# Attention with a depthwise convolution on one core: key stacks on another DMA queue, and query and key parts made at other points

## The chip, the cores and the metric

The kernel runs on one core of one Trainium2 chip. The metric is the device time of one execution in microseconds (us). A core has engines that run on their own and meet at semaphores: TensorE (PE in the profile; its weight loads are PEld), VectorE (DVE), ScalarE (ACT), GpSimd (POOL) and SyncE (SP). SP only issues DMA transfers; ScalarE and GpSimd can issue them too, each on its own queue.

## The reference

```
B, C, H, W = 4, 384, 48, 48;  N = 2304;  8 heads of 48
local   = batchnorm(depthwise_conv7x7(x))              # per channel
q, k, v = layernorm(x) @ qkv_w.T + qkv_b               # over channels, per token
q       = q + layernorm(local)
attn    = softmax(q @ k.T * 48**-0.5)                  # per head, 2304 x 2304
out     = x + (attn @ v) @ proj_w.T + proj_b           # in the layout of x
```

## The kernel before

**Tiling.** An image's 2304 tokens are cut into 6 groups of 384 tokens (8 rows of 48 pixels). There are 24 groups in all, t = 0 to 23, image b = t // 6, group g = t % 6. Heads are taken in 4 pairs; a pair fills 128 partitions, 64 for each head. Channels 0 to 287 in packed form give pairs 0 to 2, and the fourth pair is gathered from the 16 last rows of each half of the three chunks, the "tails".

**A group** is 12 slots, s = 0 to 11. Slot s belongs to pair s // 3 and to third s % 3 of the keys. `score_batch` makes six score blocks (key blocks of 128 by 384 queries) with three products for each head, and `nc.scalar.activation` takes their exponential; `weigh_batch` multiplies the six blocks with the values and sums them. The sums are copied out of PSUM by ScalarE (`sums_out`) and added by VectorE one slot later (`sums_add`). All products, scores and sums share four PSUM buffers of two banks.

**Scores from two parts.** Queries and keys are split into a high part, rounded to the faster format, and the low part that is left. For a query pair, `high_queries` casts on ScalarE (L745), `low_queries` subtracts on VectorE (L750), and SP then copies rows within the tile `qs` (L755, L757) so that 64 partitions hold the wanted combination. For keys, `stacks[b, p]` (tile `ks`, two buffers) is a pair's stack of 2 x 2304 columns. In the first group of an image the stack of the next pair is put together from the DRAM tensor `keys` by eight transfers (`stack_head`), and `keep_stack` writes the finished stack to DRAM (`wide`). In later groups `load_keys` reads it back in three pieces of 768 KB, one in each slot of the pair before. All these are issued on ScalarE's queue, after the six exponentials of the slot.

**The convolution** is 147 VectorE instructions for each group (49 taps times 3 chunks, L288). It runs one group and more ahead, in small portions between the other work: `convolve(...)` issues the portion that `plan` gave to that point. `plan` shares the instructions out by the room that `spare` and `spare_at_keys` state for each half slot, and by due points: all of group t's convolution must be issued by the first norm slot of group t - 1.

**The norm of the next group's queries** goes through slots too: `norm_slots(t)` gives (first, second), which are (6, 9) for t > 0 and (8, 10) for t = 0. The sum over channels is made one slot before `first` and sent out through DRAM (`parts`, `four`), the mean is taken off in `first`, squares are summed in the slot after it, the variance comes in `second`, and in slot `second + 1` stand `local_end` and `query_end`, which finish the queries in `xn`; `query_end` ends with `gather_tails`, eight small SP transfers into `qt`. Behind it, in the same slot, come `high_queries(t + 1, 0)` and, after the slot's second convolution portion, `low_queries(t + 1, 0)`. For the other pairs both stand in the middle slot (third 1) of the pair before.

**Before images 1 to 3** there is a key stage ("kv"), in which `from_x` makes values, keys and queries of the image's six groups and, beside them, the output projections of the image before. It is a generator; `both` takes two steps of it, the products of two items and then what reads them. For a key, the second step casts the high part on ScalarE (L592), makes the low part on VectorE (L593) and issues its transfers. The first part of the program (the prologue) does the same for image 0.

**Order.** TensorE, VectorE and ScalarE execute in the order of the program text. The orders on SP and GpSimd are set by the framework's scheduler.

Of the kernel before, what the change touches and what calls it, by code (L numbers as in the profile page):

```python
# [24 lines left out]
BATCH = 6  # L25
# [20 lines left out]
def unshifted_pass(  # L46
# [263 lines left out]


    def norm_slots(t):
        return (6, 9) if t else (8, 10)

    def spare(t, s, half):
        b, g = divmod(t, NG)
        first, second = norm_slots(t)
        time = 3.6 - (0.0 if half else 0.6) - (0.6 if half and s % 3 == 1 else 0.0)
        if b + 1 < B and g >= later(b + 1):
            time -= {(3, 1): 2.3, (4, 1): 2.2, (5, 1): 2.3, (7, 0): 0.4, (8, 0): 2.6}.get(  # L320
                (s, half), 0.0
            )
        if g:
            time -= {(2, 0): 0.7, (4, 1): 1.4}.get((s, half), 0.0)
        if t == 0:
            time -= {(7, 1): 1.1, (8, 1): 1.4, (9, 1): 1.1, (11, 0): 5.0}.get((s, half), 0.0)
        elif t + 1 < NT:
            time -= {(5, 1): 2.3, (6, 1): 2.2, (7, 1): 2.3, (9, 0): 0.4, (10, 0): 4.5}.get(
                (s, half), 0.0
            )  # L330
        return max(0.3, time)
# [37 lines left out]
    def convolve(*point):  # L369
        for _ in range(share[point]):  # L370
            next(stream)
# [143 lines left out]
                )  # L515

    keys, values = {}, {}

    def keys_out(b, g, u, k):
        at = slice(g * G, (g + 1) * G)  # L520
# [26 lines left out]

    def keep_stack(b, p):
        wide[b, p] = dram.tile([P, 2, N], F32, tag=f"wide{p}", name=f"wide{b}_{p}")
        nc.scalar.dma_start(out=wide[b, p], in_=stacks[b, p].bitcast(F32))  # L550

    def load_keys(b, p, i):
        if i == 0:
            place_keys(b, p)
        if (b, p) in wide:
            at = slice(i * BATCH * P, (i + 1) * BATCH * P)
            nc.scalar.dma_start(
                out=stacks[b, p].bitcast(F32)[:, :, at], in_=wide[b, p][:, :, at]
            )
        elif i == 0:  # L560
            for j in range(2):
                stack_head(b, p, j, keys[b][2 * p + j], slice(0, N), nc.scalar)

    def from_x(b, g, before=None, ao=None):


        src = xn[b, g]
        flat = big.tile([P, NB * NH * HA + 64 - HA], F32, tag=f"v{g}", name=f"v{b}_{g}")
        v = flat[:, 0 : NB * NH * HA].rearrange("p (t h d) -> p t h d", t=NB, h=NH)
        values[b, g] = flat  # L570
        if g == 0:
            keys[b] = dram.tile([NH, HD, 2, N], F32, tag="keys", name=f"keys{b}")
        nc.gpsimd.memset(v[:, :, :, HD:HA], 1.0)
        nc.gpsimd.memset(flat[:, NB * NH * HA :], 0.0)
        queries_of_group = []

        def value(blk, r):
            project(
                r[:, :C],
                lambda c: src[:, c, blk * P : (blk + 1) * P],  # L580
                lambda c: w_v[:, c, :],
            )
            yield
            nc.scalar.copy(v[:, blk, :, 0:HD], r[:, :C].rearrange("p (h d) -> p h d", d=HD))  # L584
            yield

        def key(u, r):
            project(r[:, :G], lambda c: w_qk[:, c, 1, u, :], lambda c: src[:, c, :])
            yield
            bias = qkb[:, 1, u : u + 1]  # L590
            k = work.tile([P, 2, G], HALF, tag="pt", name=f"k{b}_{g}_{u}", bufs=5)
            nc.scalar.activation(k[:, 0, :], r[:, :G], AF.Identity, bias=bias)  # L592
            nc.vector.scalar_tensor_tensor(  # L593
                k[:, 1, :], r[:, :G], bias, k[:, 0, :], ALU.add, ALU.subtract
            )
            keys_out(b, g, u, k)
            yield

        def query(u, r):
            project(r[:, :G], lambda c: w_qk[:, c, 0, u, :], lambda c: src[:, c, :])  # L600
            queries_of_group.append(r)
            yield
            if u == CC - 1:
                for i, q in enumerate(queries_of_group):
                    nc.scalar.activation(  # L605
                        src[:, i, :], q[:, :G], AF.Identity, bias=qkb[:, 0, i : i + 1]
                    )
            yield

        def output(co, r):  # L610
            project(r[:, :G], lambda c: w_o[:, c, co * P : (co + 1) * P], lambda c: ao[:, c, :])
            yield
            finish(before, co, r[:, :G])
            yield

        todo = [(value, i) for i in range(NB)] + [(key, i) for i in range(CC)]
        todo += [(query, i) for i in range(CC)]
        if ao is not None:
            todo += [(output, i) for i in range(CC)]
        while todo:  # L620
            r = two_banks()
            steps = [f(i, r[:, j, :]) for j, (f, i) in enumerate(todo[:2])]
            todo = todo[2:]
            for _ in range(2):
                for step in steps:
                    next(step)
                yield

    def both(making):
        next(making)  # L630
        next(making)


# [90 lines left out]
    def query_end(t):  # L724

        acc = accs.pop(t)
        q = xn[divmod(t, NG)]
        q3 = work.tile([P, G], F32, tag="qt", name=f"qt{t}", bufs=1)
        queries[t] = q, q3
        for c in range(CC):  # L730
            nc.vector.scalar_tensor_tensor(  # L731
                q[:, c, :], acc[:, c, :], gain[:, c : c + 1], q[:, c, :], ALU.mult, ALU.add
            )
        gather_tails(q3, q)

    stacked = {}

# [278 lines left out]
    query_end(0)  # L1016
    high_queries(0, 0)
    low_queries(0, 0)
    nc.vector.tensor_add(pb, pb, added)
    plan(n_first - (each - PE_TAPS))  # L1020

    for t in range(NT):
        b, g = divmod(t, NG)
        if g == 0 and b:
# [4 lines left out]
            for gk in range(NG):  # L1029
                before = t - NG + gk  # L1030
                load_residual(before)
                making = from_x(b, gk, before, ao if gk < NG - 1 else outputs[before][0])
                new = NG - later(b) + gk if gk < later(b) else None
                old = norms_x.get(gk - 1)
                both(making)
                convolve("kv", t, gk, 0)
                if new is not None:
                    norms_x[gk] = Norm(xn[b, new])
                    norms_x[gk].sum()
                    norms_x[gk].out()  # L1040
                both(making)
                if old:
                    old.few_variance()
                    old.few_root()
                if gk == 1:
                    query_end(t)
                    rb = divide(t - 1)
                if gk == 2:
                    last_ao = outputs[t - 1][0]
                    nc.vector.tensor_mul(last_ao, last_ao, rb)  # L1050
                convolve("kv", t, gk, 1)
                both(making)
                convolve("kv", t, gk, 2)
                if new is not None:
                    norms_x[gk].few_centre()
                    norms_x[gk].squares()
                both(making)
                convolve("kv", t, gk, 3)
                if old:
                    old.scale(old.few_newton())  # L1060
                both(making)
                convolve("kv", t, gk, 4)
                if new is not None:
                    norms_x[gk].sum_squares()
                    norms_x[gk].out()
                both(making)
                if gk == NG - 2:
                    high_queries(t, 0)
                if gk == NG - 1:
                    low_queries(t, 0)  # L1070
                if gk < NG - 2:
                    ao = fetch(before + 1)
        following = t + 1 < NT
# [1 line left out]
        coming = next_image and g >= later(b + 1)  # L1075
        first, second = norm_slots(t)
        for s in range(NSLOT):
            score_batch(t, s)
            pair, third = divmod(s, KB // BATCH)
            if g == 0 and third == 1:  # L1080
                keep_stack(b, pair)
            if pair < NP - 1 or g < NG - 1:
                load_keys(b, (pair + 1) % NP, third)
            if third == 1 and pair < NP - 1:
                high_queries(t, pair + 1)
            if s == 2 and g:
                rb = divide(t - 1)
            if s == 0 and coming:
# [35 lines left out]
            if s == first and t == 0:  # L1124
                norm.centre()
            weigh_batch(t, s)
            convolve("slot", t, s, 1)
            if third == 1 and pair < NP - 1:
                low_queries(t, pair + 1)
            if following and s == second + 1 and g < NG - 1:  # L1130
                low_queries(t + 1, 0)
            if coming and s == X_SLOTS[0]:
                norm_x.few_centre()
            if t and following and s == first:
# [580 lines left out]
```

## Time and profile before

| | |
|---|---|
| median of 3 runs | 3061.16 us (3057.5 to 3064.53) |
| the profiled execution | 3060.85 us |
| its span, first to last instruction | 3059.1 us |
| TensorE busy | 2832.8 us, 93% |
| VectorE busy | 2475.5 us, 81% |
| ScalarE busy | 1655.3 us, 54% |
| GpSimd busy | 14.9 us |
| mean granted TensorE clock | 0.959 |
| ScalarE's queue (q10) | 258.44 MB, 28.6% of 16 DMA engines |
| SP's queue (q1) | 169.80 MB, 22.3% of 16 DMA engines |

The span falls into a prologue (to 193 us), group 0, groups 1 to 5, and then three times a key stage of 146 to 153 us with six groups behind it; four projections stand at the end, to 3059 us. Busy shares are means over all of these. A row of the waits names the engine that waits, its line and tile, and after the arrow what ended the wait: "PE r L873 <- DMA qs<-qs" is TensorE waiting at a score product for a copy inside `qs`. In the timeline, SPq and ACTq are the issues of transfers on these queues, and the brackets hold the idle time in front of a row.

### The profile page before, as it was taken

To read this page: it belongs to the slowest core of one execution; us is meant where nothing else is said; L and a number is where in the kernel's file an instruction comes from. 1 tells how busy PE (TensorE), PEld (TensorE's weight loads), DVE (VectorE), ACT (ScalarE), POOL (GpSimd) and SP (SyncE) were. 2 spreads that over 40 slices of the span, in tenths; PEclk is the share of its full clock that TensorE was granted. 3 is DMA by queue.
4 is the path that set the end of the run, shared out by engine and by line. 5 is a ranking of instruction groups with operands and counts; after the bars stand their busy time and mean duration, and the time that the engine had idled before them with its cause. 6 is when DMAs were issued, how large, how long until landed. Compare 5 with 4: busy or idle time off the path is not lost.

```text
span 3059.1 us, 52436 instructions
## 1 busy us (share of the span) xinstructions
PE 2832.8 (93%) x19190; PEld 1788.7 (58%) x19190; DVE 2475.5 (81%) x4899; ACT 1655.3 (54%) x2638; POOL 14.9 (0%) x77
## 2 busy tenths in 40 slices
PE   8878899999998899999899879999999989999999
PEld 5445555665555556666565546666665555666665
DVE  6778999999888689988799868888878967887612
ACT  4335565666423566666542446666662256666663
POOL 1000000000000000000000000000000000000000
PEclk9979999999999899999999889999999989999999
DMA  6247544454445755446535575455463466544552
GB/s 129 50 103 189 146 123 136 140 159 130 127 124 131 179 171 149 140 136 157 153 98 134 138 189 145 142 148 144 131 174 97 128 159 185 150 142 148 166 171 84
DMA packets 222412, 431.70 MB, mean 141 GB/s; under 512 B 62592, under 2 KB 139328, under 8 KB 217024
## 3 DMA queue, kind: packets, MB, share of 16 engines
q10 hardware_dynamic: 75184, 258.44, 28.6%
q1 hardware_dynamic: 146416, 169.80, 22.3%
q8 instruction: 154, 2.52, 0.4%
q14 instruction: 114, 0.93, 0.1%
q0 software_dynamic: 544, 0.01, 0.0%
HBM read 298.44 MB, written 86.02 MB: 126 GB/s over the span
## 4 chain that ended last, share of the span: by engine, by line
PE 51%; DVE 25%; DMA 17%; ACT 2%; SPq 2%; issue 2%; ACTq 1%; DVEq 0%
PE r L873 19%; PE o L888 19%; DVE acc L288 15%; PE r L507 12%; DMA qs<-qs 6%; DMA qt<-xn 3%; DMA ks<-keys 3%; DMA parts<-part 2%; DMA four<-parts 2%; DVE xn L731 1%; ACT pt L881 1%; DVE acc L722 1%; DMA slab<-in_x_dram 1%; DVE sq L405 1%; DVE sq L404 1%
## 5 line engine op out<-in xcount | busy, mean ns | idle before, releaser
L288 DVE SCALAR_TENSOR_TENSOR acc<-slab,vec,acc 128x368 f32<-128x368 f32 (+6 forms) x3447 | 1767.8, 584 | 1.2
L881 ACT ACTIVATE pt<-r 128x768 f32<-128x768 f32 x1728 | 1261.2, 826 | 307.3 <-PE r L873 266.4
L873 PE MATMUL r<-qs,ks 64*128 64x384 f32 x10368 | 1077.3, 356 | 189.0 <-DMA qs<-qs 103.5
L888 PE MATMUL o<-pt,v 128*64 128x384 f32 x6912 | 1183.4, 492 | 0.0
L873 PEld LDWEIGHTS r<-qs,ks 64*128 64x128 f32 x10368 | 955.6, 196 | 389.1 <-issue 227.5
L888 PEld LDWEIGHTS o<-pt,v 128*64 128x64 f32 x6912 | 473.6, 137 | 592.8 <-issue 506.3
L507 PE MATMUL r<-xn,w_qk 128*128 128x384 f32 x864 | 293.1, 498 | 0.0
L773 ACT COPY o<-o 113x384 f32<-113x384 f32 x192 | 92.0, 479 | 325.4 <-PE o L888 308.9
L507 PEld LDWEIGHTS r<-xn,w_qk 128*128 128x128 f32 x864 | 169.4, 196 | 120.9 <-issue 11.8
L750 DVE TENSOR_TENSOR qs<-xn,qs 128x384 fp32r<-128x384 f32 x72 | 40.0, 556 | 217.9 <-ACT qs L745 217.9
L507 PE MATMUL r<-w_v,xn 128*128 128x384 f32 x432 | 149.1, 498 | 5.3 <-DVE xn L502 4.7
L783 ACT COPY ao<-o 113x384 f32<-113x384 f32 x72 | 34.6, 481 | 191.8 <-PE o L888 154.1
L584 ACT COPY v<-r 128x384 f32<-128x384 f32 x72 | 32.1, 481 | 186.5 <-PE r L507 186.5
L507 PEld LDWEIGHTS r<-w_v,xn 128*128 128x128 f32 x432 | 82.9, 194 | 66.5 <-DVE xn L502 6.5
L507 PE MATMUL r<-af,w_o 128*128 128x384 f32 x360 | 119.1, 487 | 0.0
L792 DVE TENSOR_TENSOR ao<-ao,o 113x384 f32<-113x384 f32 x144 | 79.5, 552 | 29.2 <-ACT o L773 29.2
L593 DVE SCALAR_TENSOR_TENSOR k<-r,qkb,k 128x384 fp32r<-128x384 f32 x72 | 44.3, 616 | 68.5 <-ACT k L592 65.7
L507 PEld LDWEIGHTS r<-af,w_o 128*128 128x128 f32 x360 | 68.2, 190 | 47.8 <-issue 0.6
L470 DVE TENSOR_REDUCE few<-four 128x12 f32<-128x48 f32 x80 | 18.5, 231 | 91.5 <-DMA four<-parts 91.3
L592 ACT ACTIVATE k<-r,qkb 128x384 fp32r<-128x384 f32 x72 | 42.0, 583 | 89.2 <-PE r L507 39.8
L750 DVE TENSOR_TENSOR qs<-qt,qs 128x384 fp32r<-128x384 f32 x24 | 13.3, 556 | 70.3 <-ACT qs L745 70.3
L605 ACT ACTIVATE xn<-r,qkb 128x384 f32<-128x384 f32 x72 | 39.3, 577 | 46.9 <-PE r L507 45.8
(119 smaller groups left out, 901.4 us busy)
## 6 DMA issues: line engine op xcount, KB each, us to landing
ks<-wide ACTq DMA_DIRECT2D x240, 768.0 KB
wide<-ks ACTq DMA_DIRECT2D x16, 2304.0 KB
qs<-qs SPq DMA_DIRECT2D x528, 48.0 KB
keys<-k SPq DMA_DIRECT2D x96, 144.0 KB
ks<-keys ACTq DMA_DIRECT2D x48, 288.0 KB
xr<-in_x_dram SPq DMA_DIRECT2D x24, 576.0 KB
slab<-in_x_dram SPq DMA_DIRECT2D x32, 378.0 KB
held<-ao SPq DMA_DIRECT2D x20, 576.0 KB
```

Of the source, the lines that this page charges most:

```text
L288: nc.vector.scalar_tensor_tensor(dst, src, weight, dst, ALU.mult, ALU.add)
L507: nc.tensor.matmul(dst, lhsT=weights(c), rhs=src(c), start=c == 0, stop=c == CC - 1)
L592: nc.scalar.activation(k[:, 0, :], r[:, :G], AF.Identity, bias=bias)
L593: nc.vector.scalar_tensor_tensor(k[:, 1, :], r[:, :G], bias, k[:, 0, :], ALU.add, ALU.subtract)
L605: nc.scalar.activation(src[:, i, :], q[:, :G], AF.Identity, bias=qkb[:, 0, i : i + 1])
L750: nc.vector.tensor_sub(qs[:, 1, :], query_of(t, p), qs[:, 0, :])
L773: nc.scalar.copy(part[0 : 64 + HA], sums[0 : 64 + HA, 0, :G])
L783: nc.scalar.copy(dst[0 : 64 + HA], sums[0 : 64 + HA, 0, :G])
L792: nc.vector.tensor_add(dst, dst, part[0 : 64 + HA])
L873: nc.tensor.matmul(r[:, j, :G], lhsT=ks[rows, w, kb * P : (kb + 1) * P], rhs=qs[rows, m, :], start=i == 0, stop=i == 2,)
L881: nc.scalar.activation(pt, r[:, :, :G], AF.Exp, scale=SCALE)
L888: nc.tensor.matmul(sums[halves[j], 0, :G], lhsT=values[t // NG, kb // NB][:, first : first + 64], rhs=pt[:, j, :], start=i == 0, stop=i == ...
```

## The change

- `keep_stack` and `load_keys` issue on GpSimd's queue instead of ScalarE's.
- `norm_slots` gives (5, 8) for t > 0, and the table in `spare` moves with it.
- In a middle slot, `high_queries` stands ahead of `score_batch` and so ahead of the exponentials; `low_queries` stands ahead of the slot's second convolution portion.
- `gather_tails` leaves `query_end` and stands behind the low part of the first pair's queries.
- In the key stage, query 0's high part is made after group 1 and its low part after group 2, instead of after groups 4 and 5.
- A key's low part and its transfers are kept in a list, `lows`, and made by the next call of `both`, after the first step of the next items.

```diff
     def norm_slots(t):
-        return (6, 9) if t else (8, 10)
+        return (5, 8) if t else (8, 10)
...
         elif t + 1 < NT:
-            time -= {(5, 1): 2.3, (6, 1): 2.2, (7, 1): 2.3, (9, 0): 0.4, (10, 0): 4.5}.get(
+            time -= {(4, 1): 2.3, (5, 1): 2.2, (6, 1): 2.3, (8, 0): 0.4, (9, 0): 4.5}.get(
...
     def keep_stack(b, p):
-        nc.scalar.dma_start(out=wide[b, p], in_=stacks[b, p].bitcast(F32))
+        nc.gpsimd.dma_start(out=wide[b, p], in_=stacks[b, p].bitcast(F32))
...
         if (b, p) in wide:
-            nc.scalar.dma_start(
+            nc.gpsimd.dma_start(
                 out=stacks[b, p].bitcast(F32)[:, :, at], in_=wide[b, p][:, :, at]
             )
         elif i == 0:
             for j in range(2):
-                stack_head(b, p, j, keys[b][2 * p + j], slice(0, N), nc.scalar)
+                stack_head(b, p, j, keys[b][2 * p + j], slice(0, N), nc.gpsimd)
...
             nc.scalar.activation(k[:, 0, :], r[:, :G], AF.Identity, bias=bias)
-            nc.vector.scalar_tensor_tensor(
-                k[:, 1, :], r[:, :G], bias, k[:, 0, :], ALU.add, ALU.subtract
-            )
-            keys_out(b, g, u, k)
+            def low():
+                nc.vector.scalar_tensor_tensor(
+                    k[:, 1, :], r[:, :G], bias, k[:, 0, :], ALU.add, ALU.subtract
+                )
+                keys_out(b, g, u, k)
+            lows.append(low)
...
     def both(making):
+        due = list(lows)
+        lows.clear()
         next(making)
+        for low in due:
+            low()
         next(making)
...
-        gather_tails(q3, q)
...
     high_queries(0, 0)
     low_queries(0, 0)
+    gather_tails(*reversed(queries[0]))
...
                 both(making)
-                if gk == NG - 2:
+                if gk == 1:
                     high_queries(t, 0)
-                if gk == NG - 1:
+                if gk == 2:
                     low_queries(t, 0)
+                    gather_tails(*reversed(queries[t]))
...
         for s in range(NSLOT):
+            pair, third = divmod(s, KB // BATCH)
+            if third == 1 and pair < NP - 1:
+                high_queries(t, pair + 1)
             score_batch(t, s)
-            pair, third = divmod(s, KB // BATCH)
...
-            if third == 1 and pair < NP - 1:
-                high_queries(t, pair + 1)
...
             weigh_batch(t, s)
-            convolve("slot", t, s, 1)
             if third == 1 and pair < NP - 1:
                 low_queries(t, pair + 1)
+            convolve("slot", t, s, 1)
             if following and s == second + 1 and g < NG - 1:
                 low_queries(t + 1, 0)
+                gather_tails(*reversed(queries[t + 1]))
```

More of the change, by code (lines that the diff above doesn't have):

```diff
@@ L517, in unshifted_pass @@
     keys, values = {}, {}
+    lows = []
     def keys_out(b, g, u, k):
```

## The prediction

> **What bounds the kernel now.** I read the busy line and the slices first, then the waits, then the stages one by one.
>
> ```profile
> PE 2832.8 (93%) x19190; PEld 1788.7 (58%) x19190; DVE 2475.5 (81%) x4899; ACT 1655.3 (54%) x2638; POOL 14.9 (0%) x77
> ...
> PEclk9979999999999899999999889999999989999999
> ```
>
> ```profile
> DVE qs L750 <- ACT qs L745: 288.2, 58, 18.7
> PE r L873 <- DMA qs<-qs: 103.5, 47, 8.4
> DVE few L470 <- DMA four<-parts: 91.3, 31, 9.8
> DVE k L593 <- ACT k L592: 65.7, 41, 8.6
> PE r L416 <- DVE sq L405: 25.0, 8, 5.3
> PE r L873 <- DVE acc L288: 23.1, 3, 9.1
> SPq L757 <- DMA ks<-keys: 143.4, 28, 13.6
> ```
>
> Columns: total us, times, longest. TensorE waits for the copies inside a query tile (qs<-qs); VectorE waits for ScalarE's cast of the high parts (L745); SP, which issues those copies, is itself held until transfers from ScalarE's queue (ks<-keys) have landed. Now five stages (prologue, key stage before image 1, its first group t=6, a later group, one of image 0):
>
> ```profile
> 18.00:193.00 175.00, 138.15 (x414) 78.24 (x412) 126.58 (x234) 55.51 (x117) 0.00 (x0) 0.89 0.37 77
> 815.00:967.00 152.00, 141.31 (x432) 82.44 (x431) 137.33 (x265) 34.98 (x72) 0.16 (x2) 0.98 0.43 113
> 967.00:1083.00 116.00, 99.58 (x720) 65.64 (x720) 84.82 (x166) 62.67 (x94) 0.00 (x0) 0.90 0.73 185
> 1926.00:2019.00 93.00, 90.60 (x726) 58.65 (x725) 83.82 (x165) 61.84 (x95) 0.00 (x0) 0.98 0.46 137
> 319.00:418.00 99.00, 93.26 (x720) 60.54 (x720) 96.27 (x189) 61.33 (x93) 0.00 (x0) 0.95 0.48 132
> ```
>
> After the length come PE, PEld, DVE, ACT, POOL, clock, DMA share, GB/s. An undisturbed slot lasts 7.36 us between its first score products, so a group of 12 has a floor of 88.3. Image 0 is bound by VectorE (96 of 99). Later images have 84 us of VectorE work per group, under the floor: there TensorE's pauses are the loss. The key stage is near both limits. A typical pause, at a group's end:
>
> ```profile
> 1914.80 5.17 SPq L513 DMA_DIRECT2D qt<-xn  x8
> 1920.09 0.52 SPq L757 DMA_DIRECT2D qs<-qs  x1
> ...
> 1923.05 2.10 SPq L757 DMA_DIRECT2D qs<-qs  x2
> ```
>
> ```profile
> 1918.67 3.39 PE L873 MATMUL r<-qs,ks 64*128 64x384 f32 x36
> ...
> 1926.02 0.79 PE L873 MATMUL r<-qs,ks 64*128 64x384 f32 x5
> 1929.21 2.19 PE L873 MATMUL r<-qs,ks 64*128 64x384 f32 x14 [2.40 <-DMA qs<-qs]
> ```
>
> Eight tail gathers go first on SP, the query copies end at 1925.2, and the group that could start at 1926.0 runs on at 1929.2.
>
> **The change, part by part.** Sums are made against the profiled execution, 3060.85 us; the median of the runs, 3061.16, is the same to 0.3.
>
> *Query norm one slot earlier, gathers behind the low parts.* The whole chain of query_end, cast, low part and copies moves 7.36 us ahead. At the boundary above the last copy was about 3.2 us late, so it is now some 4 early, even if the gathers stay ahead on SP (SP's order is not bound to the text: at 315.48 two L757 precede the L750 that stands before them). The price of such a pause is more than its length: 14 products took 2.19 us after it, 0.156 each, against 3.39/36 = 0.094 before, and slot 0 of that group lasts 11.75 instead of 7.36: 4.39 for a gap of 2.40. The Trainium skill ("TensorE: Matmul & The Clock Gate", "What's actually happening") has the clock halve only after an idle window of about 3.4 us. By that rule the twelve groups t=7-10, 13-16 and 19-22 lose only their gaps, 33.9 us, by the rows the excess of their slots, 1109.6 - 12 x 88.3 = 50.0. The rows decide; I take back 42, as VectorE's 84 leaves only 4 of play. In the same way t=11, 17, 23 are 26.2 over the floor (here residual and x loads crowd SP too): 16.
>
> *The plan of the convolution* gets an earlier due slot. Working its formula through for both versions, group 0 issues 202 instructions instead of 192, group 1 168 for 165, group 22 51 for 62. Ten at 0.51 us (1767.8/3447) cost group 0 5 us, as VectorE bounds it. Slot 4 of groups that also carry an x norm now holds about 9.5 us of VectorE work (2.3 + 2.2 + 1.4 by the plan's own table, 0.55 of sums, six convolutions); the slots behind it have fewer, so the lag should not reach ScalarE's squares two slots on.
>
> *Image starts.* The high part of query 0 moves from the key stage's fifth group to its second, the low part from the sixth to the third. TensorE's waits of 7.76, 9.10 and 6.19 us before t=6, 12, 18 (the DVE acc L288 row, 23.1) go: 21. What VectorE still owes then runs into those groups, whose VectorE idles 31 to 40 us. The tile is held longer in its pool of five beside residuals and fetched outputs; four are left for two of each, enough.
>
> *Low parts of keys behind the next products.* Here 65.7 us of VectorE waits go, but TensorE decides. In the key stages its other gaps are small (3.3 us of 153): 3 for three stages. In the prologue norm means wait for sums that stand behind the low parts: 25.0 us in L416, of which I take 15; the gathers behind the copies give 2 more (six issues, 3.70 us, go first today).
>
> *High parts ahead of the exps, low parts ahead of the convolution.* The cast (0.55 us) falls into ScalarE's wait for the first scores (10.40 us idle before it at 196.72, 0.3 in steady slots), so at worst 0.3 x 72 = 20 us were at stake and I take 0: four score buffers cover it. The copies leave 4 to 5 us earlier.
>
> *Keys' stacks on GpSimd's queue.* Removed: 352 issues and their waits on ScalarE's queue. In t=6 the copies for slot 3 were issued at 984.79 to 990.84, three of them only once ks<-keys had landed; the trace's packets show ScalarE's queue moving 4719 KB from 976.9 to 998.5 without a break and SP's copies moving only from 991.8. In t=12 ScalarE itself stood in the queue, and slot 7 lasted 22.22. Groups 6, 12, 18 are 91.6 over the floor; with their own waits gone and the copies earlier I take 55, since the 4.7 MB per pair still fill 21.6 of 22 us. Group 0 has 17.9 of VectorE idle; I take 15, less the 5 above: 10. Groups 1 to 5, bound by VectorE, have 25.3 of idle, half of it the norm's own round trip (L470): 8.
>
> Added: 240 loads of 768 KB, 16 stores, 96 smaller reads on GpSimd. The trace has only tiny ones there:
>
> ```profile
> 1.84 0.74 POOL L171 DMA_DIRECT2D of_ln<-in_ln_pair_dram  x1
> 2.57 1.52 POOL L173 DMA_DIRECT2D of_ln<-in_ln_pair_dram  x3
> ```
>
> 0.51 to 0.74 us each, by number of runs. Bounds for a load of 256 runs: 0.5, and 0.74 x 256/96 = 2.0; I take 1.2. Twelve per group are 14 us of 88 on an idle engine. Moving 786 KB took 3.05 us, so three pieces take 9 of the 22 that a pair lasts. The rule that speaks against it is the Trainium skill's "SBUF — State Buffer", "SBUF: two separate sides": software-made descriptors starve while VectorE runs a two-port op, 620 ns becoming 3100. Five times 1.2 is 6 us per load, 72 per group: still hidden. In groups 0, 6, 12, 18, with 24 reads (3 each), 4 stores and 3 loads (6 each), it is 114, and the 55 would be lost: 2944 in all. But the same page ("Who interferes with whom") lets an op with two SBUF inputs collide only with GpSimd's reads, and that is L288, 584 ns for 368 elements. No trace here shows either. I take no starvation.
>
> GpSimd's queue also carries the memsets of the value tiles, which wait for the last weighing of an image; nothing is loaded behind them before the next image, so nothing queues there.
>
> **Sum:** 42 + 16 + 21 + 3 + 17 + 55 + 10 + 8 = 172; 3061 - 172 = 2889.
>
> **Rivals.** *(a) VectorE takes over, 2975, 0.18.* The pauses go, but the chains (L470's round trip, ScalarE's waits for sums) move one step on and give half back, 86. For it: 96 of 99 in image 0. Against: 84 of 93 later. *(b) Slower, GpSimd's queue as the bound, 0.11.* If a load holds GpSimd longer than a slot, 7.36 us, stacks come late. The loads that matter fill about 20 groups of 94 us with 12 each; the other edits still give about 70, so it decides from (94 + 3.5)/12 = 8.1 us on; at 9 us it is 3061 - 70 + 20 x 14 = 3271. For it: large loads were never seen there. Against: 0.51 to 0.74. *(c) The edits do nothing, 3061, 0.03:* SP's and GpSimd's order is not the text's, so gathers may stay ahead; but the earlier slot and ScalarE's freed queue do not hang on it.
>
> **Numbers.** The likeliest case (0.68) is 2889, its own range 2835 (226 of the 254 that the excesses, waits and idle times named above make: 91.6 + 50.0 + 26.2 + 23.1 + 25.0 + 17.9 + 25.3, less 5) to 2935. Up to 2990 the range takes in (a) and the starved case; (b) stays out. About 0.2% (6 us) is what these runs can tell from no change. Faster 0.86, same 0.03, slower 0.11.
>
> **What would show it.** Slot 0 of t=7 to 22 near 7.4; no L873 row on qs<-qs above 30 us; L750's wait on L745 under 100; no SP wait on ks; L416's wait under 12; clock near 0.98; POOL busy 300 to 600 us. Wrong if POOL is busy most of the span, if score products wait for ks, or if L792 or L470 have taken L750's place while slots stay over 8 us.

## The result, and the profile after

The changed kernel takes 2953.61 us (median of 4 runs, 2949.92 to 2959.41), the one before 3059.33 (3049.21 to 3064.53) beside it: a ratio of 0.966 [0.963, 0.969]. That is faster, inside the range of 2835 to 2990, but 65 us above the 2889 of the forecast. The profiled execution took 2951.98 us, its span is 2950.2 and its mean granted clock 0.970. Added code moves the lines: the score products are now L881, the high cast L753, the low part L758, the copies L763 and L765, the key's parts L593 and L596.

Stage by stage, from the first score product of one group to that of the next, in the two profiled executions (us):

| stage | before | after | change | term of the forecast |
|---|---|---|---|---|
| prologue | 193.0 | 185.0 | -8.0 | -17 |
| group 0 | 126.1 | 119.1 | -7.0 | -10 |
| groups 1 to 5 | 495.7 | 516.3 | **+20.6** | -8 |
| three key stages | 446.9 | 419.9 | -27.0 | -24 (21 + 3) |
| groups 6, 12, 18 | 356.5 | 335.9 | **-20.6** | -55 |
| the 12 groups 7-10, 13-16, 19-22 | 1109.5 | 1067.3 | -42.2 | -42 |
| groups 11, 17, 23 | 291.1 | 266.7 | -24.4 | -16 |
| projections at the end | 40.3 | 40.0 | -0.3 | 0 |
| sum | 3059.1 | 2950.2 | -108.9 | -172 |

So the question for the experiments is where the 63 us between the two sums went: two rows, groups 1 to 5 and the first groups, make 63 of it by themselves (28.6 and 34.4).

The busy line and the clock of the page after:

```profile
PE 2783.3 (94%) x19190; PEld 1749.7 (59%) x19190; DVE 2474.2 (84%) x4899; ACT 1641.8 (56%) x2638; POOL 244.9 (8%) x429
...
PEclk9989999999999999999999989999999999999999
```

TensorE lost 50 us of busy time with the same 19190 instructions: fewer pauses, so fewer products at the lower rate behind them. The old boundary shows that rate: the granted clock was 1.00 up to the gap of 2.40 us, and the record of the clock has 0.5 from 1929.7 to 1933.1, 3.4 us, behind it. Its waits (total us, times, longest):

```profile
DVE few L470 <- DMA four<-parts: 167.6, 38, 24.6
DVE qs L758 <- ACT qs L753: 77.6, 29, 16.2
PE r L881 <- DMA qs<-qs: 67.8, 23, 8.2
...
DVE k L596 <- ACT k L593: 22.8, 18, 4.1
```

The low parts' wait for the cast fell from 288.2 to 77.6, the score products' wait for the copies from 103.5 to 67.8, the keys' from 65.7 to 22.8, and SP's 143.4 for ScalarE's transfers is gone. But the first row nearly doubled, from 91.3 to 167.6: VectorE waits at L470 for the round trip of the norm's sums through DRAM. The five stages that were shown of before (prologue, key stage, first group, a later group, one of image 0; length, then busy times, clock, DMA share, GB/s):

```profile
18.00:185.00 167.00, 130.43 (x414) 75.15 (x412) 134.75 (x250) 54.19 (x116) 4.55 (x9) 0.89 0.50 108
820.00:961.00 141.00, 139.75 (x436) 81.92 (x432) 130.27 (x252) 35.08 (x72) 0.74 (x3) 1.00 0.46 124
961.00:1072.00 111.00, 94.29 (x722) 59.26 (x720) 85.75 (x168) 61.84 (x94) 18.03 (x33) 0.94 0.82 211
1865.00:1953.00 88.00, 88.00 (x720) 56.65 (x720) 82.41 (x162) 60.85 (x94) 8.67 (x12) 1.00 0.49 154
305.00:405.00 100.00, 93.90 (x717) 60.23 (x719) 92.55 (x182) 60.94 (x93) 8.66 (x12) 0.94 0.41 120
```

The key stage and the later group have TensorE busy almost without a break (139.75 of 141 us and 88.00 of 88) at full clock. The first group is still 23 over the floor of 88.3, with the DMA engines 82% busy. In the group of image 0, VectorE is busy 92.55 of 100 where it was 96.27 of 99: that stage got worse by idling.

The boundary that paused before, now (SP, then TensorE):

```profile
1847.79 8.67 SPq L513 DMA_DIRECT2D qt<-xn  x7
...
1859.04 1.84 SPq L765 DMA_DIRECT2D qs<-qs  x2
```

```profile
1857.84 3.39 PE L881 MATMUL r<-qs,ks 64*128 64x384 f32 x36
...
1865.18 3.41 PE L881 MATMUL r<-qs,ks 64*128 64x384 f32 x36
```

The gathers still go ahead of the copies, but the last copy is issued by 1860.9, 4.3 us before the next group starts (1925.15 and 0.85 us before), and the 36 products of that slot follow without a gap in 3.41 us. The new transfers on GpSimd (issues: busy us, mean ns, idle before; then KB each and median us to landing):

```profile
L558 POOL DMA_DIRECT2D ks<-wide x240 | 173.6, 725 | 1723.4 <-PE r L881 1658.4
```

```profile
ks<-wide POOLq DMA_DIRECT2D x240, 768.0 KB, 7.0
...
wide<-ks POOLq DMA_DIRECT2D x16, 2304.0 KB, 12.1
```

One load occupies GpSimd for 0.725 us, under the 1.2 that was taken. GpSimd stands idle in front of them until score products free a buffer.

### The profile page after: what moved, and what is told of

Its sections match the earlier page's. It is cut to its first block, busy times and chain, and to the rows that moved or that the text cites. A ratio compares the mean times of both kernels' runs of the same rounds, so it can differ in the third digit from the quotient of the medians.

```text
span 2950.2 us, 52742 instructions
## 1 busy us (share of the span) xinstructions
PE 2783.3 (94%) x19190; PEld 1749.7 (59%) x19190; DVE 2474.2 (84%) x4899; ACT 1641.8 (56%) x2638; POOL 244.9 (8%) x429
## 4 chain that ended last, share of the span: by engine, by line
PE 67%; DVE 21%; DMA 10%; SPq 1%; issue 1%; ACT 1%; ACTq 0%; DVEq 0%
PE o L896 27%; PE r L881 23%; PE r L507 16%; DVE acc L288 14%; DMA parts<-part 4%; DMA four<-parts 2%; DMA qs<-qs 1%; DMA keys<-k 1%; DMA xn<-in_x_dram 1%; DVE ao L800 1%; DMA ks<-k 1%; DVE sq L405 0%; DVE qs L758 0%; DVE sq L456 0%; DVE sq L404 0%
## 5 line engine op out<-in xcount | busy, mean ns | idle before, releaser
L881 PE MATMUL r<-qs,ks 64*128 64x384 f32 x10368 | 1037.1, 349 | 137.1 <-DMA qs<-qs 67.8
L881 PEld LDWEIGHTS r<-qs,ks 64*128 64x128 f32 x10368 | 922.5, 191 | 330.0 <-issue 252.0
L558 POOL DMA_DIRECT2D ks<-wide x240 | 173.6, 725 | 1723.4 <-PE r L881 1658.4
L507 PE MATMUL r<-xn,w_qk 128*128 128x384 f32 x864 | 283.7, 486 | 0.0
L470 DVE TENSOR_REDUCE few<-four 128x12 f32<-128x48 f32 x80 | 18.6, 232 | 167.8 <-DMA four<-parts 167.6
L507 PE MATMUL r<-af,w_o 128*128 128x384 f32 x360 | 119.1, 487 | 0.0
L791 ACT COPY ao<-o 113x384 f32<-113x384 f32 x72 | 34.4, 478 | 122.8 <-PE o L896 122.8
L758 DVE TENSOR_TENSOR qs<-xn,qs 128x384 fp32r<-128x384 f32 x72 | 39.9, 555 | 70.4 <-ACT qs L753 70.4
L593 ACT ACTIVATE k<-r,qkb 128x384 fp32r<-128x384 f32 x72 | 39.4, 580 | 63.4 <-PE r L507 51.8
L862 DVE SCALAR_TENSOR_TENSOR xr<-r,pb,xr 128x384 f32<-128x384 f32 x72 | 42.1, 612 | 35.8 <-PE r L507 20.0
## 6 DMA issues: line engine op xcount, KB each, us to landing
wide<-ks POOLq DMA_DIRECT2D x16, 2304.0 KB, 12.1
```

What stands on the lines that cost most here:

```text
L507: nc.tensor.matmul(dst, lhsT=weights(c), rhs=src(c), start=c == 0, stop=c == CC - 1)
L558: nc.gpsimd.dma_start(out=stacks[b, p].bitcast(F32)[:, :, at], in_=wide[b, p][:, :, at])
L758: nc.vector.tensor_sub(qs[:, 1, :], query_of(t, p), qs[:, 0, :])
L862: nc.vector.scalar_tensor_tensor(xr[:, co, :], m, pb[:, co : co + 1], xr[:, co, :], ALU.add, ALU.add)
L881: nc.tensor.matmul(r[:, j, :G], lhsT=ks[rows, w, kb * P : (kb + 1) * P], rhs=qs[rows, m, :], start=i == 0, stop=i == 2,)
```

## The experiments

Stage lengths are always of the one profiled execution. Stages that an edit doesn't touch scatter a little (the prologue, unchanged in text, was 182.4 to 185.5 us in four kernels and 179.5 in `slot6`), so differences of 3 us in a stage are not read, and in the prologue none under 6. Groups 8 to 10 stand at an edge: they are at the floor of 88.3 in the changed kernel, but take 89 to 97 us each in seven of the others, mostly with edits elsewhere. So the twelve middle groups vary between 1059 and 1086 us among the kernels with the earlier slot, and this is named where it matters. The profiled executions of `no_lows` and `fill5` are the slowest of their five, 14 and 12 us above the median.

**The queue and the slot, apart.** Four kernels make a square: `acts_queue` is the changed kernel with the stacks back on ScalarE's queue, `pool_only` is the kernel before with only the queue changed, and `slot6` undoes only the norm's slot.

```diff
# acts_queue, on the changed kernel, in keep_stack and load_keys
-        nc.gpsimd.dma_start(out=wide[b, p], ...)
+        nc.scalar.dma_start(out=wide[b, p], ...)
...
# pool_only, on the kernel before: the reverse
# slot6, on the changed kernel (with the old table in spare)
-        return (5, 8) if t else (8, 10)
+        return (6, 9) if t else (8, 10)
```

> All of the change but the queue: stacks on ScalarE's queue again. Burst theory (the three pieces of a stack, let go together on GpSimd's queue, delay the norm's round trip through DRAM): VectorE's wait on four<-parts falls from 167.6 to about 90 us and groups 1 to 5 from 516 to about 495; the groups that begin an image lose what the free queue gave them (336 for t=6, 12, 18 goes back to 350 or more). Total 2940 to 2965. Slot theory (the earlier norm slot alone makes the round trip late): four<-parts stays above 150 and groups 1 to 5 above 510.

> The kernel before with nothing but the stacks on GpSimd's queue. My sum gave the queue 55 us in the groups that begin images 1 to 3. The boundary pauses of the other groups stay (slot 0 near 11.5). Burst theory: four<-parts above 120 us, first groups 20 to 30 us shorter in all, groups 1 to 5 some 10 longer: total 3035 to 3050.

> All of the change but the norm slots, which are (6, 9) again with the table of before. Slot theory: four<-parts back under 100 us, groups 1 to 5 near 495, total about 2935. Burst theory: the sums leave at the end of slot 5, into the pieces that start with slot 6, so four<-parts stays above 150 and the total is 2950 to 2970. Either way the pauses at group boundaries of images 1 to 3 should stay small, since the gathers are behind the copies: if they come back (over 3 us each), it was the slot that removed them.

Measured: `acts_queue` 2970.29 us, 0.9703 [0.966, 0.9746]; `pool_only` 3178.64, 1.0387 [1.0341, 1.0432]; `slot6` 3032.72, 0.9916 [0.9889, 0.9943]. The queue alone costs 119 us, and on top of the other edits it brings 17: 2953.6 against 2970.3, with intervals that overlap. The earlier slot is worth 79 us here (3032.7 - 2953.6). No total was as expected: `acts_queue` lies 5 us above its range, with groups 1 to 5 (503.7) between the two theories, `slot6` 63 above the higher of its two, `pool_only` 129 above its range.

By stages, the excess of slot 0 of the twelve middle groups over 7.36 us is 46.2 before, 8.0 after, 6.6 in `acts_queue`, and 50.8 in `slot6`: the slot alone removes the pauses at the boundaries, whatever the queue. In `pool_only` it is 46.4, and slot 11 adds 75.8 (20.4 in `slot6`). One such end of a group in `pool_only`:

```profile
2081.85 2.16 POOL L557 DMA_DIRECT2D ks<-wide  x3 [22.34 <-PE r L873]
2083.48 0.53 SPq L757 DMA_DIRECT2D qs<-qs  x1
...
2086.01 1.23 SPq L757 DMA_DIRECT2D qs<-qs  x2
2091.77 0.65 PE L873 MATMUL r<-qs,ks 64*128 64x384 f32 x1 [6.21 <-DMA qs<-qs]
```

The last score products of pair 3 free a stack, and GpSimd, which waited only for that, sends all three pieces of 768 KB at once. On ScalarE's queue they stood one in each slot, in the order of the text. The late query copies are issued 1.6 us behind them and land late: TensorE waits 6.21 us. With the earlier slot those copies are out before the pieces are let go (1860.9 against 1861.54 at the boundary shown above). That is the interaction at the boundaries. The starts of images 1 to 3 lose in the same place: TensorE's waits before t=6, 12 and 18 are 17.7, 20.3 and 19.0 us in `pool_only`, against 7.8, 9.1 and 6.2 before. These 34 us are the whole growth of its key stages (480.8 against 446.9); where query 0 is made earlier, as in `slot6`, the key stages are 420.1 on the same queue. A third loss, 19.2 us in groups 1 to 5, is not cured by early copies.

In groups 1 to 5, VectorE bounds: its busy time there is 466 to 470 us in every kernel, so its idle time decides. Its wait at L470 in these groups:

| L470's idle, groups 1-5 (us) | slot 6 | slot 5 |
|---|---|---|
| ScalarE's queue | 13.7 (before) | 28.5 (`acts_queue`) |
| GpSimd's queue | 31.1 (`slot6`) | 46.0 (after) |

Slot about +15, queue about +17, and in the idle time they add. `pool_only`, with the queue and none of the other edits, has 30.3, which agrees with the queue's share. In the length of the stage they do not add: it is 495.7 before, 503.7 in `acts_queue`, 513.0 in `slot6` and 516.3 after, so the queue adds 17.3 or 12.6 us and the slot 8.0 or 3.3. The queue has the larger part of the loss.

**Why the round trip is longer on GpSimd's queue: the three pieces at once?** In a group of image 0 after the change (group 2):

```profile
454.22 0.60 SPq L460 DMA_DIRECT2D parts<-part  x1
455.35 2.17 POOL L558 DMA_DIRECT2D ks<-wide  x3 [29.24 <-PE r L881]
457.66 0.58 SPq L461 DMA_DIRECT2D four<-parts  x1
467.03 0.24 DVE L470 TENSOR_REDUCE few<-four 128x12 f32<-128x48 f32 x1 [8.31 <-DMA four<-parts]
```

The sums leave at 454.22, three loads start 1.1 us later, and the means can be taken at 467.03. `paced` holds pieces 2 and 3 of a stack back by a one-column copy on GpSimd that reads the slot's exponentials, so that they go one in each slot. `wide_image0_act` sends image 0's loads, and the stores, on ScalarE's queue.

```diff
# paced, in load_keys
             at = slice(i * BATCH * P, (i + 1) * BATCH * P)
+            if i:
+                nc.gpsimd.tensor_copy(
+                    stacks[b, p][:, 0, at.start : at.start + 1],
+                    weighing[-1][3][:, 0, 0:1],
+                )
...
# wide_image0_act, in load_keys (and the store as in wide_act)
-            nc.gpsimd.dma_start(
+            (nc.gpsimd if b else nc.scalar).dma_start(
                 out=stacks[b, p]...
```

> The changed kernel with pieces 1 and 2 of each reloaded stack held until the slot's last exponential, by a one-column GpSimd copy from that slot's weights ahead of the transfer, so that one piece leaves in each slot as it did on ScalarE's queue. Burst theory: four<-parts under 110 us, groups 1 to 5 near 495, total about 2925. Queue theory (any traffic on GpSimd's queue beside SP's small transfers makes them late, however spread): no change, 2945 to 2960.

> The changed kernel with the stores, and the reloads of image 0 alone, on ScalarE's queue. With the whole change but the queue groups 1 to 5 took 503.7 against 516.3; if the reloads on GpSimd's queue cost image 0 that much by delaying the norm's round trip, groups 1 to 5 come to about 504 and the total to 2917 - 13 = 2904. If it was chance, they stay at 515 to 519.

Measured: `paced` 2949.89, 0.9651 [0.9605, 0.9698]; `wide_image0_act` 2908.69, 0.9506 [0.9476, 0.9536]. Pacing took 5.6 us off L470's idle in groups 1 to 5 (46.0 to 40.4), a third of the queue's 17, and the median moved by less than its interval (the first groups gain 14.3, to 321.6, and groups 8 to 10 give 10.3 back). So the burst explains only a part of it: the stage (511.0) and the total are nearer to the queue theory. With image 0's loads on ScalarE's queue the idle is 28.2, as in `acts_queue`, and the stage 500.5 (about 504 expected): the queue's part is confirmed, its mechanism is not settled beyond the burst's third.

**Why it is longer in slot 5: the output's store?** The output projection of the image before stands in slot 4, as the sums now do, and its transfers (`held<-ao`, issued 0.5 us before the sums at 454.22) share SP with them. `out7` moves it to slot 7.

```diff
-OUT_SLOT = 4
+OUT_SLOT = 7
...
-            time -= {(2, 0): 0.7, (4, 1): 1.4}.get((s, half), 0.0)
+            time -= {(2, 0): 0.7, (7, 1): 1.4}.get((s, half), 0.0)
```

> The changed kernel with OUT_SLOT 7 instead of 4 (and its 1.4 us moved in the table): the 576 KB store of held<-ao no longer stands on SP just ahead of the norm's sums. Held-store theory (the earlier slot made the round trip late because the sums now leave behind that store): VectorE's wait on four<-parts in groups 1 to 5 falls from 46.0 to about 31 us and these groups from 516 to about 501; total about 2938. If the store has nothing to do with it, groups 1 to 5 stay above 511.

Measured: 2954.08, 0.9663 [0.9636, 0.9691], no gain as a whole. L470's idle in groups 1 to 5 falls from 46.0 to 38.2, half of the slot's 15, and the stage from 516.3 to 508.5; the middle groups give 5.7 back and group 0 3.1. So the stage lies between what the two theories said (501 and 511), and the rest of the slot's share stays open.

**Whatever lengthens it, is it only unfilled time?** VectorE executes in order; if convolution is put in front of L470 it has something to do. The plan gives slot 5 of groups 1 to 5 only 6 to 10 convolution instructions. `fill5` adds room to the plan at the point between the sums and L470, and the plan then gives 14 to 21.

```diff
# fill5, at the end of spare
+        if 0 < t < NG and (s, half) == (5, 1):
+            time += 5.2
         return max(0.3, time)
```

> The changed kernel with 5.2 us more room in the plan for slot 5's second half in groups 1 to 5, so that 14 to 21 convolution instructions instead of 6 to 10 stand between the norm's sums and the read that waits for them. Fill theory (image 0 is bound by VectorE, and it got slower because VectorE now arrives early at a round trip of some 12 us and stands in order): the wait on four<-parts in these groups falls from 46.0 to 20 or less, the groups from 516 to about 492, all else unchanged, total about 2930. Rival (the round trip itself, by what SP and the rings carry, makes them late, and later arrival only moves the pause to ScalarE's squares and TensorE): groups 1 to 5 stay above 508.

Measured: 2939.4, 0.9601 [0.9574, 0.9628]. L470's idle in groups 1 to 5 goes from 46.0 to 22.3, the stage from 516.3 to 494.9, and VectorE's busy time stays (468.7). In the trace of groups 1 to 3, 17 or 18 convolution instructions stand between the sums and L470, where the change has 7 or 8. This one row of a table takes back the stage's loss: the round trip costs what the plan leaves unfilled in front of it. All else was not unchanged: the total fell by 14 only (2930 expected), and in the profiled execution, one of the slow end, group 0, the first groups and the middle groups are 5.2, 3.8 and 11.6 us longer.

**The first groups: the store of a whole stack.** In the first group of an image `keep_stack` writes 2304 KB for each pair. Group 6 after the change:

```profile
999.87 0.60 SPq L460 DMA_DIRECT2D parts<-part  x1
...
1000.80 0.54 POOL L551 DMA_DIRECT2D wide<-ks  x1 [9.29 <-DMA ks<-keys]
...
1026.31 0.58 SPq L461 DMA_DIRECT2D four<-parts  x1
1028.48 0.23 DVE L470 TENSOR_REDUCE few<-four 128x12 f32<-128x48 f32 x1 [24.65 <-DMA four<-parts]
```

The store starts as soon as its stack has landed, 0.93 us behind the sums' small write, and that write is not through until 1026.31, 26 us after its issue; VectorE stands for 24.65 of it, and ScalarE's squares and the next queries behind VectorE. The store itself has landed at 1012.84. From 1013 to 1026.3 GpSimd's queue moved a further 1.9 MB, its reads of the next stack (issued from 1006.62 on), and SP's queue 0.16 MB; so the store has the first half of these 26 us, and the second half comes with the reads behind it. `wide_act` moves the 16 stores alone back to ScalarE's queue, where they stand behind the exponentials of their slot.

```diff
# wide_act, in keep_stack, on the changed kernel
-        nc.gpsimd.dma_start(out=wide[b, p], in_=stacks[b, p].bitcast(F32))
+        nc.scalar.dma_start(out=wide[b, p], in_=stacks[b, p].bitcast(F32))
```

> The changed kernel with the 16 stores of whole stacks (wide<-ks) back on ScalarE's queue, reads left on GpSimd's. Run-ahead theory (GpSimd's queue lets the 2.3 MB store go as soon as its data are there, ahead of the small copies and sums that the first groups wait for): the prologue ends at about 170 instead of 185, VectorE's wait on four<-parts in t=6, 12, 18 falls from 20 to 25 us each to about 10, these groups from 336 in all to 315 or less; total about 2918. Rival (the reads crowd the rings, or the store does it from any queue): first groups stay above 330, and holds on SP's copies by the shared semaphores return.

Measured: 2917.29, 0.9522 [0.9485, 0.9558], 36 us better than the change. The same place in its trace:

```profile
996.17 0.60 SPq L460 DMA_DIRECT2D parts<-part  x1
999.23 0.33 ACTq L551 DMA_DIRECT2D wide<-ks  x1
999.55 0.57 SPq L461 DMA_DIRECT2D four<-parts  x1
1008.24 0.24 DVE L470 TENSOR_REDUCE few<-four 128x12 f32<-128x48 f32 x1 [5.98 <-DMA four<-parts]
```

The sums are written in 3.4 us, and the wait is 5.98. Over groups 6, 12 and 18 the time from the sums' write to the issue of the read behind it is 11.5 us on average after the change and 6.7 in `wide_act` (two round trips in each group; 26.4 is the longest). L470's idle in these groups, 26.6 us before, is 69.3 after and 41.3 in `wide_act`. The three groups go from 335.9 to 295.6 us, or 60.9 under before. `acts_queue`, with the whole stack on ScalarE's queue, has 354.1: the gain needs loads and head pieces on GpSimd, and the store off it.

The prologue may show the same thing once more. After the change, its end reads:

```profile
162.04 0.56 POOL L551 DMA_DIRECT2D wide<-ks  x1 [149.56 <-DMA keys<-k]
171.51 0.58 SPq L763 DMA_DIRECT2D qs<-qs  x1
...
179.38 1.76 SPq L765 DMA_DIRECT2D qs<-qs  x2
184.98 0.65 PE L881 MATMUL r<-qs,ks 64*128 64x384 f32 x1 [20.86 <-issue]
```

and in `wide_act`:

```profile
169.39 0.53 SPq L763 DMA_DIRECT2D qs<-qs  x1
...
171.87 1.22 SPq L765 DMA_DIRECT2D qs<-qs  x2
```

The first queries' copies end at 181.1 behind the store, and at 173.1 without it; the prologue is 185.0 and 179.3 us (169.9 in `acts_queue`), where about 170 was expected. The four kernels with the store alone on ScalarE's queue have 176.6 to 179.3; but `slot6`, with the store on GpSimd's, has 179.5 too, so the store's share of the prologue is not cleanly told from scatter. Groups 8 to 10 are off the floor here, 94.2 to 96.2 us, with a long slot 7 of 12 to 15 us each.

**The two small edits.** `no_lows` makes a key's low part at once, as before; `gathers_first` puts `gather_tails` back into `query_end`.

```diff
# no_lows
-            lows.append(low)
+            low()
...
# gathers_first, at the end of query_end; the three later calls leave
+        gather_tails(q3, q)
```

> The changed kernel with a key's low part and its transfers made at once again, as before. My sum gave this edit 3 us in the key stages and 15 in the prologue: total about 2971, TensorE's wait in L416 back near 25 us, key stages 420 to 425. Rival (the key stages' gain of 27 came from this edit and not from the earlier query 0): key stages above 435.

> The changed kernel with gather_tails back inside query_end, ahead of the copies. With the earlier slot the copies are about 4 us early even so, and I gave the order 2 us in the prologue: 2950 to 2960, slot 0 of images 1 to 3 at 7.4. Rival (the order is what removed the boundary pauses): 3 us or more per boundary come back, total above 2990.

Measured: `no_lows` 2974.13, 0.9717 [0.969, 0.9744]; `gathers_first` 2959.25, 0.9683 [0.9649, 0.9716]. The order of the gathers is worth nothing that this can tell; without the later low parts the kernel is 20 us slower. In `no_lows` the three key stages are 430.8 us (419.9 after; 420 to 425 expected), 8.4 of the 10.9 in the first of them, and the prologue 189.3 (185.0), which makes 15; groups 8 to 10, which the edit doesn't touch, are 19.9 longer, and the first groups 2.8 shorter. So what can belong to the edit is about 15, and the prologue's 4.3 of it is inside the scatter. The prologue's wait is back near its old 25, where the change leaves one wait of 1.1:

```profile
PE r L416 <- DVE sq L405: 24.0, 7, 5.3
```

With `gathers_first`, slot 0 of the middle groups has an excess of 5.5 us: the boundaries do not pause. Its prologue of 189.6 is 4.6 longer than after's, as much as in `no_lows`, and neither is read.

**A version that beats both.** Two combinations of what the runs had shown: `wide_fill` is `fill5` with `wide_act`, and `wide_fill_out7` adds `out7`.

```diff
# wide_fill: the edits of fill5 and wide_act; wide_fill_out7: and of out7
```

> Stores of whole stacks on ScalarE's queue and the fuller slot 5 together. If the two causes are apart, their gains add: 2917 - 24 = 2893; first groups 296, groups 1 to 5 near 493.

> The same with OUT_SLOT 7 as well. OUT_SLOT alone took 8 us from groups 1 to 5 and gave some back elsewhere; with slot 5 filled the wait that it shortened is mostly gone: 2885 to 2895, no more than 6 us under the run without it.

Measured: `wide_fill` 2901.96, 0.948 [0.9456, 0.9504]; `wide_fill_out7` 2872.0 (2870.37 to 2879.19), 0.9393 [0.9369, 0.9417], the fastest of all. Its span is 2868.3, its clock 0.983. Groups 1 to 5 take 487.6 us, the first groups 300.7, and the twelve middle groups 1059.3, which is their floor of 12 times 88.3. Its waits:

```profile
DVE few L472 <- DMA four<-parts: 95.4, 29, 10.5
...
PE r L883 <- DMA qs<-qs: 33.0, 13, 9.8
```

L470 (here L472) is back near the 91.3 of before, and the copies hold TensorE for 33.0 us of the 103.5 of before. Both totals missed what was expected: `wide_fill` by 9 us upward, `wide_fill_out7` by 13 downward. The output's move, worth nothing by itself and expected to give 6 at most, is worth 30 us behind the two others: `wide_fill` has groups 7 to 10 at 93.7, 92.6, 94.4 and 95.0 us, and the move brings all four to 88.3 (in `out7` groups 8 to 10 are there too); another 8.1 come in groups 1 to 5. That the output's work in slot 4, on top of the norm's, is what pushes these groups over their edge is inferred from this; which wait carries it was not tried apart.

## Why the prediction was right, and where it failed

The total was inside the range because the range was wide: 2953.6 is 65 us above the likeliest case and 21 under rival (a)'s 2975, which the range took in.

**Middle groups, 42 forecast, 42.2 measured.** The mechanism held: TensorE no longer waits at the boundary, and `slot6` brings the pauses back (50.8 us of excess) while `acts_queue` doesn't (6.6). The play was less than said. "Some 4" was the time from the last copy's landing to the group's start; at the boundary shown 4.3 us lie between the end of its issue and that start, and before the change TensorE ran on 4.06 us after that issue ended. The issue moved by 3.5 us there and not by 7.36, as seven of the gathers ahead of the copies took 8.67 us on SP. That SP's order is not that of the text also held: the gathers stay ahead and cost nothing, and `gathers_first` is not told apart from the change. In the rows, one pause of 2.40 us at the old boundary had cost 4.39, and the granted clock was 0.5 for 3.4 us behind that gap, which the cited rule, with its idle window of about 3.4 us, does not give for one of 2.40. So the stage's 42.2 exceeds the 33.9 of bare gaps that the rule left. The floor would have given 50 (`wide_fill_out7`), and kernels with groups 8 to 10 off it give as little as 24 (`no_lows`, 1085.8): 42 is inside a band, not a constant of the edit.

**Last groups, 16 forecast, 24.4 measured.** The forecast took part of their excess to be residuals and x loads that crowd SP; they went to 266.7, 1.8 above three floors.

**Image starts and key lows, 24 forecast, 27.0 measured,** with the parts mis-sized: `no_lows` puts the low parts at 10.9 us in the key stages, where 3 was taken from TensorE's small gaps, so some 16 of the forecast 21 are left for the earlier queries. That is a difference and not a run: the earlier query 0 was not undone by itself. That VectorE's wait counts in a stage near two limits, although TensorE's gaps look small, is the likely reason; no run shows it apart.

**First groups, 55 forecast, 20.6 measured.** The failed step is "with their own waits gone and the copies earlier I take 55". The waits behind ScalarE's queue went, but the forecast costed GpSimd's transfers by their issue alone. A store on a queue that runs ahead of the text met the norm's round trip, and L470's idle there rose from 26.6 to 69.3 us. The 55 itself could be had: with the store moved off, the stage gains 60.9.

**Groups 1 to 5, 8 gained in the forecast, 20.6 lost.** The failed step is counting half of the 25.3 us of idle as "the norm's own round trip" and then moving that norm without asking what lies in front of it. Slot and queue lengthened L470's idle by 15 and 17, on an engine that bounds this stage; of the stage's length the queue has the larger part, and why it lengthens the trip is open but for the burst's third. `fill5` shows that the price is the plan's empty slot: 21.4 us back by one line. This is rival (a)'s mechanism, "L470's round trip", confined to image 0 and the first groups. The forecast had named the sign of it ("if L792 or L470 have taken L750's place"); it came true here and not in the middle groups, which reached their floor.

**Prologue, 17 forecast, 8.0 measured.** L416's wait fell to 1.1, as forecast (under 12). The term left out the store issued at 162.04 ahead of the copies; without it the prologue gains 13.7, and 23.1 with the loads on ScalarE's queue too, though the first of these differences is near the scatter.

**Group 0, 10 forecast, 7.0 measured;** the difference is within the scatter. Its cost term is not seen in the trace: by the plan the group issues ten convolution instructions more, but between the first score products of groups 0 and 1 VectorE executes 177 of them after the change and 182 before (what runs past that point is not counted).

**GpSimd.** A load took 0.725 us instead of 1.2, GpSimd is busy 244.9 us and not 300 to 600, and no row has score products wait for `ks`. Rival (b)'s outcome, slower by GpSimd's queue, is real (`pool_only`, 1.0387), but by another way: nothing was near the 8.1 us for a load from which it decides; what cost was that its transfers are let go together and early, beside late copies. The starvation rule of the Trainium skill ("SBUF — State Buffer", "SBUF: two separate sides"), five times the price, is not seen: 725 ns for an issue with VectorE 84% busy. No run has these loads without VectorE's work beside them, so this shows only that they stayed far from the 6 us that the forecast feared.

Of the other signs, L881's row on the copies was to be under 30 us and is 67.8: 28.1 of it lies in groups 1 to 5, 17.5 in the first groups and 9.0 in group 0. The clock was to be near 0.98 and is 0.970; the last version's 0.983 is where it arrives when those stages are mended.

## What to carry to other kernels

Moving transfers to an idle engine's queue moves their times too: a queue that waits only for buffers sends bulk data as early as it can, so ask which small transfer it will then travel beside, and leave a bulk store behind an engine that is paced by the work. When an operation with a round trip is moved, what counts is the work that the plan puts between its ends; fill that gap in the same edit. And try the parts of a change singly and together: here a queue that alone costs 119 us gains 17 behind the other edits, and a move worth nothing alone was worth 30 behind two others.

## What the runs showed of the hardware

- The norm's small write on SP's queue (128 x 12 numbers) took 26 us instead of 3.4 when GpSimd's queue was given a 2304 KB store within a microsecond of it and reads of the next stack behind that, with the DMA engines 82% busy over that group. That is the longest case: over the first groups the average is 11.5 us against 6.7 in `wide_act`. The Trainium skill ("DMA: Bandwidth & Descriptors", "Issuing engines are not separate DMA queues") says that all issuers share the same 16 engines; these rows agree, since a transfer on one issuer's queue is late beside one on another's. In `pool_only` a change of the issuing engine alone cost 119 us.
- Behind a gap of 2.40 us TensorE's granted clock was 0.5 for 3.4 us (1929.7 to 1933.1 before the change); it was 1.00 up to the gap.
- GpSimd takes 0.725 us to issue a 768 KB load of 256 runs, and 0.56 for a 2304 KB store: the issue hardly depends on the bytes. The loads land after 7.0 us (median), the stores after 12.1.
- Spreading the same loads over three slots changed L470's idle by 5.6 us of 46.0 only. What else lengthens the small round trip beside GpSimd's queue stays open.
